# Feed-forward norm of a six-layer stack: by products across partitions, or token-major by transposes and statistics instructions in twelve slots

## The chip, the cores and the metric

The kernel runs on one core of a Trainium2 chip. The metric is the device time of one execution in microseconds (us). Three runs of the kernel before took 2170.97, 2175.17 and 2180.14 us, median 2175.17.

## What is computed

Four blocks follow each other on four batch elements of 512 tokens with 128 features: a linear attention, a stack of six layers, an attention with position slopes, and a gated network. The change lies in the second block. Its core in the reference:

```python
for i in range(DEPTH):            # 6
    x = attn_layer(shift_tokens(x), Wqkv[i], q_scale[i], k_scale[i], Wo[i]) + x
    x = ffn_layer(shift_tokens(x), ln_g[i], ln_b[i], W1[i], b1[i], W2[i], b2[i]) + x

def ffn_layer(x, g, bln, W1, b1, W2, b2):
    mu = x.mean(-1, keepdims=True)
    var = ((x - mu) ** 2).mean(-1, keepdims=True)
    xn = (x - mu) / jnp.sqrt(var + 1e-05) * g + bln
    a, gate = jnp.split(xn @ W1 + b1, 2, -1)
    return a * jax.nn.gelu(gate, approximate=False) @ W2 + b2
```

The attention layer has 16 heads of 64 features and windows of 32 tokens, of which each sees itself and the one before. The inner width of the feed-forward network is 341, taken as chunks of 128, 128 and 85 rows.

## The kernel before, in words

The stack keeps each batch element feature-major in a tile `z[b]`: 128 features on the partitions, the 512 tokens behind each other, the lower and the upper half of the features shifted against each other by one token (`halves`, L125).

The order of the stack is written out by hand (L643 to L705), as one loop over slots `s`; each engine runs its instructions in the order in which they are recorded. A step `k` is one half (8 heads) of one batch element in one layer, and takes four slots, one for each pair of heads. So a layer of four batch elements has 32 slots, and a group, one batch element's attention and feed-forward, has 8. In a slot the loop records, for the step that is `here`: the scores of a pair (`score`, L420: eight mask products of L429, then 32 small products of L439), the row maximum (`top`, L446, L448) on VectorE, eight exponentials with sums on ScalarE (L71 by way of L455), and at the slot's end the reciprocal (L463, VectorE) and the normalising product (L464, GpSimd). One slot later VectorE transposes the weights (L480) and SP issues eight DMAs that place them as `pT` (L490); two slots later TensorE forms the weighted values (L500), ScalarE copies them out (`attn`, L687), and in the slot after that they go through the output product (L508), which sums the eight pairs of a group in the PSUM tile `py` (L665, one buffer). Beside this, each slot does two projections of later steps (L323), whose results VectorE multiplies with the rotary table (L334) and ScalarE squares (L342); VectorE sums the squares (L354); GpSimd adds the rotated halves (L350); TensorE turns two earlier tiles (L395) and ScalarE copies the turns (L397); one value product (L405) is copied by ScalarE (`vn`, L409), and once in four slots SP moves the values (`ve`, L415 to L417). At the start of each fourth slot L363 clamps the sums and ScalarE takes a logarithm and an exponential.

PSUM: the score tile `sc` has a single buffer of two banks (L424). The products of projection, turn, value and feed-forward share four banks, tag `mm` (L287), which are given out in turn; a product waits until all readers of the tile that had its bank before are done.

The feed-forward of group g (`ff_part`, L513) is recorded at the end of the slots that follow its last output product, one part in each of seven slots. Recorded at the end of a slot, its instructions stand on each engine behind that slot's and ahead of the next slot's.

```python
done, part = divmod(s - 1, 8)
if 1 <= part and 1 <= done <= DEPTH * NB:
    ff_part(*divmod(done - 1, NB), part)
```

Part 1 (s mod 8 = 2): VectorE adds the output product to `z` (L517). Part 2 (3): TensorE multiplies by the centring matrix `cent` (L522), ScalarE takes the square (L524) and a copy with the scale g (L526). Part 3 (4): four one-column products with `mean_c` give the variance by token (L530), VectorE adds epsilon (L535), GpSimd raises to the power -0.5 (L536). Part 4 (5): four products spread it over the partitions (L540), VectorE multiplies (L545). Part 5 (6): three gate products (L550), and three gelus with a table load before and after. Part 6 (7): two up-products (L561), VectorE adds the bias and multiplies by the gelu (L565). Part 7 (0): the third one, the down-product (L571), and VectorE adds the result to `z` in two halves (L576). The next layer's projections of the same batch element begin at g*8 + 16.

The norm's own bias has no step of its own: `bias_late` (L291) multiplies it once for each layer by W1, twelve one-column products (L297), and three sums on VectorE (L304) make the six bias columns that parts 5 to 7 use. It stands in the layer's thirteenth slot (L622). `weights` (L615) records the loads of the next layer on SP; `par`, `w1` and `w2` have one buffer (L150, L617 to L621) and are loaded in the layer's tenth and eleventh slot.

In the last layer `residual` (L585) takes each batch element to the next block, in four parts after its feed-forward: GpSimd copies (L592), a centring product with square and copy (L595 to L597), the variance product with logarithm and exponential (L600 to L602), product and sum (L604, L605).

Of the kernel before, what the change touches and what calls it, by code (L numbers as in the profile page):

```python
# [32 lines left out]
def sandwich(ctx: ExitStack, tc: tile.TileContext, a: dict, out: bass.AP):  # L33
# [97 lines left out]
    with tc.tile_pool(name="a0w", bufs=1) as awp, tc.tile_pool(name="a0", bufs=4) as work, \  # L131
# [17 lines left out]
        for n in ("par", "w1", "w2"):  # L149
            loaded(0, n, a[f"f0_{n}"][0], bufs=1)  # L150
# [135 lines left out]
    with tc.tile_pool(name="f0", bufs=2) as work, \  # L286
# [4 lines left out]
        def bias_late(i):  # L291

            w = ws[i]
            pb = mm.tile([P, S], F32, tag="mm", name="pb")
            for k in range(6):
                h0, m = HCH[k % 3]
                nc.tensor.matmul(  # L297
                    pb[:m, k : k + 1],
                    lhsT=w["w1"][:, (k // 3) * DIN + h0 : (k // 3) * DIN + h0 + m],
                    rhs=w["par"][:, 5:6], start=True, stop=True,  # L300
                )
            w["bias"] = bias = wp.tile([P, 6], F32, tag="bias", bufs=1, name=f"bias_{i}")
            for c, m in ((0, P), (1, P), (2, HCH[2][1])):
                nc.vector.tensor_tensor(  # L304
                    bias[:m, c::3], pb[:m, c:6:3], w["par"][:m, 7 + c : 13 : 3], ALU.add
                )

# [91 lines left out]
        def value(k, t):  # L399
# [9 lines left out]
            nc.scalar.copy(o["vn"][:, t, :], pv)  # L409
# [100 lines left out]

        ff = {}

        def ff_part(i, b, part):  # L513
# [6 lines left out]
            elif part == 2:  # L520
                pc = mm.tile([P, S], F32, tag="mm", name="pc")
                nc.tensor.matmul(pc, lhsT=cent, rhs=zb[:, cur], start=True, stop=True)  # L522
                ff["sq"] = work.tile([P, S], F32, tag="ffsq", bufs=1, name="ffsq")
                nc.scalar.activation(ff["sq"], pc, AF.Square)  # L524
                ff["xg"] = work.tile([P, S], F32, tag="xg", bufs=1, name="xg")
                nc.scalar.activation(ff["xg"], pc, AF.Copy, scale=w["par"][:, 4:5])  # L526
            elif part == 3:
                pv = mm.tile([P, S], F32, tag="mm", name="pvar")
                for t in range(4):
                    nc.tensor.matmul(  # L530
                        pv[:, t : t + 1], lhsT=ff["sq"][:, t * P : (t + 1) * P], rhs=mean_c,
                        start=True, stop=True,
                    )
                rs = ff["rs"] = work.tile([P, 4], F32, name="rs")
                nc.vector.tensor_scalar_add(rs, pv[:, 0:4], 1e-5)  # L535
                nc.gpsimd.tensor_tensor(rs, rs, mhalf, ALU.pow)  # L536
            elif part == 4:
                pr = mm.tile([P, S], F32, tag="mm", name="prs")
                for t in range(4):
                    nc.tensor.matmul(  # L540
                        pr[:, t * P : (t + 1) * P],
                        lhsT=ff["rs"][:, t : t + 1].to_broadcast([P, P]),
                        rhs=ident, start=True, stop=True,
                    )
                nc.vector.tensor_tensor(ff["xg"], ff["xg"], pr, ALU.mult)  # L545
            elif part == 5:
                ff["gl"] = []
                for c, (h0, m) in enumerate(HCH):
# [6 lines left out]
                    table_act(gl[:m], pg[:m], AF.Gelu, bias=w["bias"][:m, 3 + c : 4 + c])  # L555
                    ff["gl"].append(gl)
            else:
                for c in ((0, 1), (2,))[part - 6]:
# [7 lines left out]
                        gl[:m], pa[:m], w["bias"][:m, c : c + 1], gl[:m], ALU.add, ALU.mult  # L566
                    )
                if part == 7:
                    py = mm.tile([P, S], F32, tag="mm", name="py")
                    for c, (_, m) in enumerate(HCH):  # L570
                        nc.tensor.matmul(  # L571
                            py, lhsT=w["w2"][:m, c, :], rhs=ff["gl"][c][:m, :],
                            start=(c == 0), stop=(c == 2),
                        )
# [576 lines left out]
```

## Time and profile before

| what | us |
|---|---|
| median of three runs | 2175.17 |
| the profiled execution | 2175.81 |
| its span, first to last instruction | 2174.1 |
| first slot's and last slot's scores begin | 127.3 and 1743.4 |
| TensorE busy | 1965.5 |
| ScalarE busy | 1671.6 |
| VectorE busy | 1574.3 |
| GpSimd busy | 1192.0 |

The profile is of one execution. PE is TensorE's products, PEld its weight loads, DVE VectorE, ACT ScalarE, POOL GpSimd, SPq the queue of SP. A line such as L446 is that of the kernel. In a row of the order in time, the first number is the start in us from the span's start, the second the duration, then engine, line, operation, output<-input, shapes, and in brackets the idle time of the engine just ahead and what ended it. A row of a stretch has the busy time of each engine and the number of its instructions, the granted TensorE clock (1.00 is full), the DMA share and GB/s. The chain is the work that ended last, followed backwards; its shares say which engine carried it.

### The profile page before, as it was taken

Reading aid. Unit: us, or ns where it says so; the run is one execution under the profiler, and the core shown is the slowest. Engines: PE = TensorE matmul, PEld = TensorE weight load, DVE = VectorE, ACT = ScalarE, POOL = GpSimd, SP = SyncE. Lnnn points to the kernel's source line nnn. Section 1 sums busy time; section 2 is a strip of 40 time slices with the busy share of each in tenths; the row PEclk is TensorE's granted clock in tenths of the full one; section 3 lists DMA queues with packets and bytes.
Section 4 is the critical chain, followed back from the end, with each engine's and each line's share of the span. In section 5 each row is a group of like instructions: output and inputs, shape, how many; then the busy total and the mean of one; then the engine's idle time right before and its main releaser. Section 6 shows DMA issues by size and latency. Waiting matters only on the chain.

```text
span 2174.1 us, 64681 instructions
## 1 busy us (share of the span) xinstructions
PE 1965.5 (90%) x25584; PEld 1098.2 (51%) x25584; DVE 1574.3 (72%) x2320; ACT 1671.6 (77%) x4786; POOL 1192.0 (55%) x1017
## 2 busy tenths in 40 slices
PE   6789999999999999999999999999999877788877
PEld 3245555555555565555555555555555533333323
DVE  3677777777777777877777777787777328888843
ACT  4477887887878788888888878888878636988973
POOL 1266566555664556645566555664555316888860
PEclk9799999999999999999999999999999987898898
DMA  2013322233221332213322133222221210000000
GB/s 91 0 36 89 96 64 74 56 91 94 65 72 52 93 96 67 72 53 95 95 65 73 52 94 95 66 72 53 80 70 53 74 36 20 1 1 1 1 0 20
DMA packets 98844, 129.40 MB, mean 60 GB/s; under 512 B 29552, under 2 KB 81520, under 8 KB 93936
## 3 DMA queue, kind: packets, MB, share of 16 engines
q1 hardware_dynamic: 98544, 125.27, 20.7%
q8 instruction: 204, 3.34, 0.7%
q14 instruction: 96, 0.79, 0.1%
HBM read 23.44 MB, written 1.05 MB: 11 GB/s over the span
## 4 chain that ended last, share of the span: by engine, by line
PE 48%; ACT 25%; DVE 16%; issue 4%; DMA 3%; SPq 3%; POOL 2%; ACTq 0%; POOLq 0%; DVEq 0%
ACT pr L71 11%; PE pp L323 8%; PE av L500 5%; PE pv L405 5%; PE py L508 4%; ACT sq L342 4%; PE tp L395 4%; PE sc L439 3%; PE py L571 3%; DMA pT<-blocks 3%; SPq L490 3%; PE pa L561 3%; ACT lb L71 2%; PE pg L550 2%; DVE la L850 2%
## 5 line engine op out<-in xcount | busy, mean ns | idle before, releaser
L350 POOL TENSOR_TENSOR r<-t 128x512 f32<-128x512 f32 x384 | 490.2, 1278 | 714.2 <-DVE t L334 601.9
L71 ACT ACTIVATE pr<-sc,top,rn 128x64 f32<-128x64 f32 x1536 | 607.9, 420 | 255.6 <-DVE top L448 233.6
L334 DVE TENSOR_TENSOR t<-pp,tab 128x1024 f32<-128x1024 f32 x384 | 466.8, 1215 | 11.1 <-PE pp L323 8.7
L354 DVE TENSOR_REDUCE ss<-sq 128x8 f32<-128x512 f32 x384 | 263.0, 685 | 227.5 <-ACT sq L342 227.3
L323 PE MATMUL pp<-wqkv,z 128*128 128x512 f32 x768 | 420.3, 631 | 6.6 <-ACT sq L342 6.3
L71 ACT ACTIVATION_READ_ACCUMULATOR pr<-sc,top,rn 128x1 f32 x1536 | 335.0, 218 | 0.0
L395 PEld LDWEIGHTS tp<-ident,r 128*128 128x128 f32 x1536 | 193.6, 142 | 206.5 <-issue 173.0
L342 ACT ACTIVATE sq<-pp 128x512 f32<-128x512 f32 x384 | 239.1, 623 | 34.6 <-DVE t L334 32.5
L395 PE MATMUL tp<-ident,r 128*128 128x128 f32 x1536 | 233.6, 275 | 0.9 <-ACT sq L342 0.9
L500 PE MATMUL av<-pT,vn 128*64 128x64 f32 x3072 | 194.0, 225 | 36.9 <-DMA pT<-blocks 36.6
L464 POOL TENSOR_TENSOR pr<-pr,den 128x512 f32<-128x512 f32 x192 | 200.7, 1045 | 45.5 <-DVE den L463 38.7
L405 PE MATMUL pv<-wqkv,z 128*128 128x512 f32 x384 | 219.4, 654 | 6.4 <-ACT sq L342 6.2
L508 PE MATMUL py<-attn,wo 128*128 128x512 f32 x384 | 200.6, 604 | 14.2 <-DVE z L517 12.5
L858 POOL TENSOR_TENSOR lb<-lb,la 128x2048 f32<-128x2048 f32 x40 | 182.2, 4556 | 53.0 <-issue 38.8
L500 PE MATMUL av<-pT,ve 128*64 128x64 f32 x3072 | 204.0, 229 | 2.7 <-DMA pT<-blocks 2.7
L380 POOL TENSOR_TENSOR r<-r,rn 128x512 f32<-128x512 f32 x192 | 197.0, 1049 | 0.0
L446 DVE TENSOR_REDUCE top<-sc 128x8 f32<-128x512 f32 x192 | 131.7, 686 | 87.2 <-PE sc L439 84.9
L323 PEld LDWEIGHTS pp<-wqkv,z 128*128 128x128 f32 x768 | 132.1, 192 | 120.2 <-issue 81.2
L500 PEld LDWEIGHTS av<-pT,vn 128*64 128x64 f32 x3072 | 161.7, 139 | 41.0 <-issue 30.9
L500 PEld LDWEIGHTS av<-pT,ve 128*64 128x64 f32 x3072 | 159.5, 138 | 38.8 <-issue 34.5
L439 PE MATMUL sc<-kT,qT 64*32 64x64 f32 x12288 | 166.3, 224 | 0.0
L439 PEld LDWEIGHTS sc<-kT,qT 64*32 64x32 f32 x12288 | 152.6, 106 | 0.0
(191 smaller groups left out, 3129.1 us busy)
## 6 DMA issues: line engine op xcount, KB each, us to landing
pT<-blocks SPq DMA_DIRECT2D x1536, 32.0 KB, 1.8
ve<-vn SPq DMA_DIRECT2D x48, 768.0 KB, 5.8
wqkv<-in_f_wqkv SPq DMA_DIRECT2D x36, 256.0 KB, 3.0
ve<-vn SPq DMA_DIRECT2D x48, 192.0 KB, 5.6
tab<-in_rot SPq DMA_DIRECT2D x12, 256.0 KB, 3.1
wo<-in_f_wo SPq DMA_DIRECT2D x6, 512.0 KB
ve<-vn SPq DMA_DIRECT2D x48, 64.0 KB, 5.2
w<-in_f_w SPq DMA_DIRECT2D x6, 341.0 KB
```

Source lines behind the costliest of these rows:

```text
L71: done = nc.scalar.activation(out, in_, func, **kw)
L323: nc.tensor.matmul(pp, lhsT=z[b][:, WIN + t * P : WIN + (t + 1) * P], rhs=ws[i]["qkv", hf][:, n * S : (n + 1) * S], start=True, stop=True,)
L334: nc.vector.tensor_tensor(t12, o["pp"].rearrange("p (h d) -> p h d", d=DH0).unsqueeze(1) .to_broadcast([P, 2, 8, DH0]), ws[i][f"tab{n}"][: ...
L342: nc.scalar.activation(sq, o["pp"], AF.Square)
L350: nc.gpsimd.tensor_tensor(r, t1, t2[:, :, ::-1, :], ALU.add)
L354: nc.vector.tensor_reduce(o["ss"][:, n, t, :], o["sq"].pop(j).rearrange("p (h d) -> p h d", d=DH0), AX.X, ALU.add,)
L395: nc.tensor.transpose(tp[:, p, :], flat[:, p * P : (p + 1) * P], ident)
L405: nc.tensor.matmul(pv, lhsT=z[b][:, WIN + t * P : WIN + (t + 1) * P], rhs=ws[i]["qkv", hf][:, 2 * S :], start=True, stop=True,)
L439: nc.tensor.matmul(scores[32 * w : 32 * w + 32, e, j, :], lhsT=o["qT"][rows, p, q0 : q0 + WIN], rhs=o["kT"][rows, p, q0 : q0 + KW], start= ...
L464: nc.gpsimd.tensor_tensor(o["pr"], o["pr"], o["den"].unsqueeze(3).to_broadcast([P, 2, 4, KW]), ALU.mult)
L500: nc.tensor.matmul(av[64 * e : 64 * e + 64, q0 : q0 + 64], lhsT=vs[c][:, j, (2 * p + e) * DH0 : (2 * p + e + 1) * DH0], rhs=pT[:, c, :, 4 ...
L508: nc.tensor.matmul(py, lhsT=ws[i]["wo"][:, c, :], rhs=t, start=(c == 0), stop=(c == 7))
```

## The change

The norm becomes token-major. Part 2 turns the four token blocks of `z` by four transposes on TensorE, and ScalarE copies them to a tile `xt` (tokens on the partitions). Part 3 takes mean and variance by four bn_stats and four bn_aggr instructions on VectorE; epsilon and power stay. The new part 4 subtracts the mean and multiplies by the norm, four instructions on VectorE. The new part 5 turns back, four transposes, and ScalarE copies out with g as scale and the norm's bias as bias. Gates, up-products and down-product follow as parts 6 to 9; the first is as before but for its bias, which comes straight from `par`. `bias_late` is gone.

Parts and the four parts of the residual have a list of their slots, counted from 8*g: 2, 3, 5, 7, 8, 9, 11, 13, 14, and 15 to 18. So two groups overlap, and by s mod 8 the parts stand at 2 (part 1), 3 (part 2 and, of the group before, part 7), 5 (3 and 8), 6 (9), 7 (4), 0 (5) and 1 (6). The loop runs five slots longer. In the slot of the gates (s mod 8 = 1) the copies `attn` and `vn` are on VectorE in place of ScalarE. `par`, `w1` and `w2` have two buffers.

```diff
-            loaded(0, n, a[f"f0_{n}"][0], bufs=1)
+            loaded(0, n, a[f"f0_{n}"][0])
...
-        def bias_late(i):
...
-            nc.scalar.copy(o["vn"][:, t, :], pv)
+            copy(o["vn"][:, t, :], pv)
...
+        LATE = (2, 3, 5, 7, 8, 9, 11, 13, 14, 15, 16, 17, 18)
...
             elif part == 2:
-                pc = mm.tile([P, S], F32, tag="mm", name="pc")
-                nc.tensor.matmul(pc, lhsT=cent, rhs=zb[:, cur], start=True, stop=True)
-                ff["sq"] = work.tile([P, S], F32, tag="ffsq", bufs=1, name="ffsq")
-                nc.scalar.activation(ff["sq"], pc, AF.Square)
-                ff["xg"] = work.tile([P, S], F32, tag="xg", bufs=1, name="xg")
-                nc.scalar.activation(ff["xg"], pc, AF.Copy, scale=w["par"][:, 4:5])
+                pt = mm.tile([P, 4, P], F32, tag="mm", name="pt")
+                for t in range(4):
+                    nc.tensor.transpose(
+                        pt[:, t, :], zb[:, WIN + t * P : WIN + (t + 1) * P], ident
+                    )
+                ff["xt"] = work.tile([P, 4, P], F32, tag="xt", bufs=1, name="xt")
+                nc.scalar.copy(ff["xt"], pt)
             elif part == 3:
-                pv = mm.tile([P, S], F32, tag="mm", name="pvar")
+                st = work.tile([P, 4, 6], F32, tag="st", bufs=1, name="st")
+                ff["mv"] = mv = work.tile([P, 4, 2], F32, tag="mv", bufs=1, name="mv")
                 for t in range(4):
-                    nc.tensor.matmul(
-                        pv[:, t : t + 1], lhsT=ff["sq"][:, t * P : (t + 1) * P], rhs=mean_c,
-                        start=True, stop=True,
-                    )
+                    nc.vector.bn_stats(out=st[:, t, :], in_=ff["xt"][:, t, :])
+                for t in range(4):
+                    nc.vector.bn_aggr(out=mv[:, t, :], in_=st[:, t, :])
                 rs = ff["rs"] = work.tile([P, 4], F32, name="rs")
-                nc.vector.tensor_scalar_add(rs, pv[:, 0:4], 1e-5)
+                nc.vector.tensor_scalar_add(rs, mv[:, :, 1], 1e-5)
                 nc.gpsimd.tensor_tensor(rs, rs, mhalf, ALU.pow)
             elif part == 4:
-                pr = mm.tile([P, S], F32, tag="mm", name="prs")
                 for t in range(4):
-                    nc.tensor.matmul(
-                        pr[:, t * P : (t + 1) * P],
-                        lhsT=ff["rs"][:, t : t + 1].to_broadcast([P, P]),
-                        rhs=ident, start=True, stop=True,
-                    )
-                nc.vector.tensor_tensor(ff["xg"], ff["xg"], pr, ALU.mult)
+                    nc.vector.tensor_scalar(
+                        ff["xt"][:, t, :], ff["xt"][:, t, :], ff["mv"][:, t, 0:1],
+                        ff["rs"][:, t : t + 1], ALU.subtract, ALU.mult,
+                    )
             elif part == 5:
+                px = mm.tile([P, 4, P], F32, tag="mm", name="px")
+                for t in range(4):
+                    nc.tensor.transpose(px[:, t, :], ff["xt"][:, t, :], ident)
+                ff["xg"] = work.tile([P, S], F32, tag="xg", bufs=1, name="xg")
+                nc.scalar.activation(
+                    ff["xg"], px.rearrange("p t c -> p (t c)"), AF.Identity,
+                    bias=w["par"][:, 5:6], scale=w["par"][:, 4:5],
+                )
+            elif part == 6:
...
-            for s in range(-8, LAST + 14):
+            for s in range(-8, LAST + LATE[-1] + 1):
...
+                copy = nc.scalar.copy
+                if s % 8 == LATE[5] % 8 and LATE[5] < s:
+                    copy = nc.vector.tensor_copy
...
-                    nc.scalar.copy(attn, av)
+                    copy(attn, av)
...
+                for part, late in enumerate(LATE, 1):
+                    g, left = divmod(s - late, 8)
+                    if left or not 1 <= g <= DEPTH * NB:
+                        continue
+                    if part < 10:
+                        ff_part(*divmod(g - 1, NB), part)
+                    elif g > NB * (DEPTH - 1):
+                        residual((g - 1) % NB, part - 9)
```

## The prediction

> **What bounds the kernel now.** I read four views in this order: busy times and chain on the page, busy time by stretch over one cycle of eight slots, the order of VectorE, ScalarE and TensorE instructions inside that cycle, and the waits. Only the stack (127 to 1743 us of the span) is touched, and the passage to the next layer behind it.
>
> ```profile
> PE 1965.5 (90%) x25584; PEld 1098.2 (51%) x25584; DVE 1574.3 (72%) x2320; ACT 1671.6 (77%) x4786; POOL 1192.0 (55%) x1017
> PE 48%; ACT 25%; DVE 16%; issue 4%; DMA 3%; SPq 3%; POOL 2%; ACTq 0%; POOLq 0%; DVEq 0%
> ```
>
> TensorE looks like the bound, but only half of the chain is its own. The second view shows why: one cycle, a row for each slot from its first mask product, here s mod 8 = 4, 5, 6, 7, 0, 1, 2, 3.
>
> ```profile
> core 0: us, PE busy (x) PEld busy (x) DVE busy (x) ACT busy (x) POOL busy (x), PEclk, DMA share, GB/s
> 900.40:907.94 7.54, 7.54 (x129) 5.18 (x129) 6.63 (x12) 7.51 (x27) 3.29 (x3) 1.00 0.14 37
> 907.94:915.50 7.56, 7.56 (x129) 5.11 (x128) 5.78 (x11) 6.59 (x24) 7.27 (x7) 1.00 0.56 156
> 915.50:926.10 10.60, 9.44 (x127) 5.24 (x126) 6.62 (x10) 9.19 (x27) 7.21 (x8) 1.00 0.22 56
> 926.10:934.50 8.40, 8.40 (x125) 4.77 (x124) 5.30 (x8) 8.37 (x26) 2.90 (x3) 1.00 0.08 22
> 934.50:944.80 10.30, 10.30 (x137) 5.46 (x138) 8.50 (x16) 7.09 (x25) 4.93 (x5) 1.00 0.14 38
> 944.80:951.70 6.90, 6.75 (x129) 4.14 (x129) 5.98 (x9) 4.26 (x19) 2.74 (x4) 1.00 0.63 164
> 951.70:959.20 7.50, 6.83 (x128) 4.22 (x128) 5.93 (x9) 6.13 (x23) 5.71 (x7) 1.00 0.15 40
> 959.20:967.60 8.40, 7.77 (x130) 4.46 (x131) 6.75 (x11) 6.31 (x23) 3.69 (x4) 1.00 0.13 34
> sum 67.20, PE 64.58 PEld 38.58 DVE 51.50 ACT 55.44 POOL 37.73; mean PE 8.07 PEld 4.82 DVE 6.44 ACT 6.93 POOL 4.72
> ```
>
> A slot without feed-forward work takes 6.68 us of TensorE by the chain's pieces (mask and scores 0.89, projections 1.06 and 0.86, two turns of 0.44, output 0.86, weighted values 1.08, value 1.05). Slots 7, 0, 4 and 5 are that plus their own products. Slots 1, 2, 3 and 6 hold 2.6 us in which TensorE waits. The third view shows what it waits for in slots 1 to 3; the lines are of VectorE, ScalarE, TensorE.
>
> ```profile
> 946.42 0.69 DVE L446 TENSOR_REDUCE top<-sc 128x8 f32<-128x512 f32 x1
> 952.62 0.69 DVE L354 TENSOR_REDUCE ss<-sq 128x8 f32<-128x512 f32 x1 [0.77 <-ACT sq L342]
> 953.23 0.68 DVE L446 TENSOR_REDUCE top<-sc 128x8 f32<-128x512 f32 x1
> 953.94 0.87 DVE L448 TENSOR_TENSOR top<-top,rn 128x8 f32<-128x8 f32 x1
> 960.72 1.37 DVE L517 TENSOR_TENSOR z<-z,py 64x512 f32<-64x512 f32 x2
> 962.13 0.69 DVE L446 TENSOR_REDUCE top<-sc 128x8 f32<-128x512 f32 x1
> ```
>
> ```profile
> 947.44 0.40 ACT L71 ACTIVATE pr<-sc,top,rn 128x64 f32<-128x64 f32 x1 [4.19 <-DVE top L448]
> 951.93 0.66 ACT L342 ACTIVATE sq<-pp 128x512 f32<-128x512 f32 x1
> ```
>
> ```profile
> 951.67 0.30 PE L429 MATMUL sc<-mask,identb 64*32 64x256 bf16 x8 [0.15 <-ACT pr L71]
> 959.16 0.30 PE L429 MATMUL sc<-mask,identb 64*32 64x256 bf16 x8 [0.67 <-ACT pr L71]
> 962.25 1.10 PE L508 MATMUL py<-attn,wo 128*128 128x512 f32 x2 [0.63 <-DVE z L517]
> ```
>
> There is a second clock, a ring of VectorE and ScalarE. The row maximum (top, at T) releases the first exponential (A = T + 1.02). ScalarE needs 5.15 from there to the end of the second square, VectorE's sum of it is behind that, and the next maximum is behind the sum: 5.79 after A, so 6.81 from top to top (946.42 to 953.23). What VectorE does at a slot's end is added: 1.4 for z at 960.72. And as the score tile is single, the next scores start 4.23 after A (951.67, 959.16). So a slot lasts the longer of TensorE's work and lag + 4.23. All my sums use these two clocks.
>
> **The change, part by part.** *TensorE products.* Taken out per group: centring 0.86, variance 0.79, spreading 0.89 (chain pieces), 2.54. Added: eight transposes. The row is the turn (L395), four of the same form in 0.44 on the chain, so 0.88; saved 1.66. The Trainium skill speaks against that (TensorE: Matmul & The Clock Gate, Part 4: PE-mode transpose): a transpose costs about 275 ns in a kernel and transposes may not hold the clock up. By it eight cost 2.2 and 0.34 is saved. The record of one turn here is 275 ns too, but four end in 0.44 and the clock column beside them reads 1.00; I take 0.88.
>
> *ScalarE and GpSimd.* Square 0.69 and scaled copy 0.78 go, a copy of 0.6 and a scaling of 0.66 come; GpSimd's power (1.03) moves from slot 4 to slot 5 and is needed two slots later: nothing, under waits of 1.3 and more in each of these slots.
>
> *Layer bias.* bias_late goes: twelve one-column products and three sums a layer. The cycles that hold it take 70.1, 68.2, 68.1, 68.0 and 70.1 us (stretches between first mask products) where plain ones take 67.15: together 9 us. The table's second buffer costs nothing: the same DMAs leave SP at the same slots, and without it their loads would wait for the later readers.
>
> *Spreading.* By slot mod 8 the feed-forward work becomes 0: back-transpose and scaling; 1: gates; 2: first sum into z; 3: transpose and two up-products; 5: statistics and third up-product; 6: down-product and z; 7: scaling by the norm. I go round once, from slot 7 (lag = T from the slot's start).
> - 7: z is written after the down-product as in slot 1 now, so lag 1.65, A 2.67, length 2.67 + 4.23 = **6.9** (TensorE 6.68 waits).
> - 0: the ring brings 8.46, then four scalings and the clamp L363 (0.37 mean). One 128-wide VectorE step: 512 wide takes 0.61 start to start (952.62 to 953.23), 0.53 of it elements, so 0.13 + 0.08 = 0.21 for 128; the scaling (SBUF only) at the rate of L765's 481 ns for 512 about 0.14. That makes 0.55. It must also pass GpSimd: L448 took 0.87 instead of 0.17 when GpSimd was busy. The Trainium skill (SBUF — State Buffer, Who interferes with whom) agrees, and says that a tensor_scalar in a two-port form is held up in the same way, for a whole GpSimd instruction. By L448's mean (0.32) one such wait is 0.15, by the rule up to 1.28 (L350); I take 0.4. T = 8.46 + 1.3 - 6.9 = 2.9, A 3.9, length **8.1** (TensorE 7.12).
> - 1: T 1.5, A 2.6 to 2.7. The second gate product takes the bank of the second projection, free after the square (A + 5.15 = 7.8; four banks in turn), restarts at 0.24 more (1.10 against 0.86 at L508): 7.85 + 0.24 + 1.72 = **9.8**. ScalarE's copies of attn and value (1.0) go to VectorE, 2 x 0.62; reciprocal and second sum queue behind them, and behind these GpSimd's normalising; all are needed only in slot 2, over 1 us later. So hidden; without that cover 1.2.
> - 2: the last gelu follows the last gate product by 0.7, then the table load 1.28: A 2.1, TensorE bound, **6.75**.
> - 3: z adds 1.4: T 2.55, A 3.6. L508 waits 0.3 with its restart. The first up-product is now third behind pv and needs the second projection's bank: 3.6 + 5.15 = 8.75, + 0.24 + 1.72 = **10.7**. TensorE's own work is 8.84: here 1.9 is lost.
> - 4: T 1.1, **6.7**. 5: T 1.3, A 2.4, **7.55**.
> - 6: statistics. The trace has no such instruction. Lower bound for one: 0.21 (128 elements), aggregate 0.09 (L535, 128x4, is 0.15 as a record). Upper: 0.5 and 0.3, two passes. I take the lower, nearest to the reduction's row: 0.84 + 0.36 + 0.1, + gl 0.67, + 0.2 port: 2.2. T = 2.4 + 5.79 + 2.2 - 7.55 = 2.85. The length stays today's: the down-product equals the gates, and the DMA wait stays (the third ve transfer holds SP's queue from 911.86 to 914.16, the pT transfers issue only from 914.27, and av waits 1.4 for them): **10.6**.
>
> Sum 67.1 against 67.2. So the 1.66 saved on TensorE, and the calmer slots 0 and 7, are spent in slots 1 and 3, where products come to banks that the ring frees late. 23 cycles x -0.1 = -2.
>
> *Passage behind the stack.* The last groups are five slots longer. Now 44.8 us pass from the last scores (1743.5) to x (1788.2). Before the last output come the third group's gates and residual product, 2.58 + 0.86 = +3.4; what they replace (pa, py at 1754 to 1759) lay under the wait for pT. From z (1764.0) to the gates (1770.8) it takes 6.8 now; then transposes 0.65, three up-products of the other group 2.6, gl 0.7, statistics 1.4, gl 0.7, down-product 1.1, z 1.5, scaling 0.8, transposes and copy 1.3: 10.8, a little of it overlapping: +3.3. The other residual's logarithm and table load come between: +2. Together +8 (bounds 3 and 11).
>
> Sum: 2175.8 - 2 - 9 + 8 = 2172.8, against the profiled execution's 2175.81 (span 2174.1, 1.7 around it); the median is 0.6 lower. So **2172**.
>
> **Rivals.** *TensorE is the bound after all*: ring and banks do not bite in 0, 1 and 3. These slots shrink to 7.3, 9.3 and 9.3, cycle 64.7, -2.5 x 23 = -57, with -1: 2117. For it: 90% busy; against: the waits of slots 1 to 3. Half of it (one of the bank waits missing) gives about 2148. *Slower: the statistics delay the maximum of slot 6.* At the upper costs slot 6 gets 2.0 + 1.2 + 0.1 + 0.67 + 0.4 = 4.4 in place of 2.2, so T 5.0, A 6.1; the value product needs the bank that the first square frees (A + 2.1 = 8.2) before 1.05 + 2.58: 11.9, +1.3 x 23 = +30: 2202. It decides from about 2.8 at the end of slot 5 on, when A + 2.1 passes 7.1, the end of today's DMA wait. *The two copies do nothing*: then slot 2 starts its exponentials 1.0 later, slot 3 too: +20, 2192.
>
> **Numbers.** Main case, within 0.5% (about what a measurement of this kernel can tell from no change, 11 us): 0.46. First rival 0.08 in full and 0.17 by half: faster 0.25. Slower by statistics 0.21, by copies 0.08: slower 0.29. The range leaves out the full first rival and little above the slow one: 2142 to 2204.
>
> **What would show it.** Slots 0 to 7 near 8.1, 9.8, 6.75, 10.7, 6.7, 7.55, 10.6, 6.9. The first up-product waits for ScalarE's square or copy, scores wait for pr in slots 7 and 0; statistics about 0.3 as records; TensorE busy some 45 us less; about 53 us from the last scores to x. I am wrong if up-products in slot 3 do not wait, if slot 6 passes 11 us, or if records of the scalings are mostly above 0.5.

## The result, and the profile after the change

The changed kernel takes 2179.8 us (median of 20 runs, 2170.3 to 2192.0), the kernel before 2175.4 (20 runs beside them): a ratio of 1.0019, 95% interval 1.0003 to 1.0034. The forecast of 2172 had the size of the change about right, next to nothing, and its sign wrong: by the interval the change costs 1 to 7 us, where 3 were to be saved. The profiled execution has a span of 2179.3 us, 5.3 more than before.

The page of the changed kernel, its busy times and the chain by engine:

```profile
PE 1924.5 (88%) x25272; PEld 1055.7 (48%) x25272; DVE 1634.9 (75%) x2611; ACT 1655.7 (76%) x4741; POOL 1191.6 (55%) x1017
PE 37%; ACT 26%; DVE 21%; SPq 5%; issue 5%; DMA 5%; POOL 1%; ACTq 0%; DVEq 0%; POOLq 0%
```

TensorE has 41 us less to do, close to the forecast (45), and its share of the chain falls from 48% to 37%. The shares that grew are those of VectorE (16% to 21%), of SP's queue (3% to 5%) and of DMA (3% to 5%). In the mean of the 23 cycles TensorE has 1.8 us less work in each, and is idle for 1.7 us more (4.6 in place of 2.9). One cycle by stretch, rows for s mod 8 = 4, 5, 6, 7, 0, 1, 2, 3, as in the forecast's table:

```profile
core 0: us, PE busy (x) PEld busy (x) DVE busy (x) ACT busy (x) POOL busy (x), PEclk, DMA share, GB/s
897.17:903.85 6.68, 6.68 (x123) 4.06 (x122) 6.20 (x11) 5.17 (x21) 1.28 (x1) 1.00 0.12 27
903.85:911.51 7.66, 7.66 (x124) 4.47 (x123) 5.98 (x10) 6.32 (x23) 6.19 (x6) 1.00 0.56 153
911.51:922.61 11.10, 9.47 (x127) 5.30 (x126) 8.03 (x19) 7.49 (x25) 8.27 (x9) 1.00 0.22 51
922.61:929.52 6.91, 6.75 (x121) 4.15 (x121) 5.95 (x9) 4.24 (x19) 1.37 (x2) 1.00 0.08 19
929.52:937.82 8.30, 7.47 (x126) 4.75 (x125) 7.42 (x16) 6.64 (x25) 3.46 (x3) 1.00 0.15 37
937.82:947.48 9.66, 9.51 (x127) 5.03 (x126) 7.78 (x13) 9.26 (x27) 7.98 (x8) 1.00 0.52 139
947.48:954.70 7.22, 6.75 (x121) 4.14 (x121) 4.54 (x7) 7.19 (x23) 3.43 (x5) 1.00 0.18 41
954.70:965.31 10.61, 9.33 (x128) 5.25 (x127) 8.22 (x13) 8.50 (x27) 5.68 (x5) 1.00 0.14 34
sum 68.14, PE 63.62 PEld 37.17 DVE 54.13 ACT 54.80 POOL 37.67; mean PE 7.95 PEld 4.65 DVE 6.77 ACT 6.85 POOL 4.71
```

TensorE is idle for 4.5 us of this cycle, most of it in slots 6, 3 and 0. Outside the first two cycles and the last, seven slots have the same length in almost every cycle (slots 4, 5, 7, 0, 1, 2, 3: 6.68, 7.6, 6.90, 8.30, 9.65, 7.22, 10.60); slot 6 alone varies, mostly from 10.1 to 11.9 (13.7 once, where the granted clock is at half for 3.4 us), with a mean of 10.9.

Where the 5.3 us come from, by the stretches between first mask products (forecast beside it). The last mask product is that of the last slot; the passage is taken to the end of the copy L590 (L597 before) of the last batch element:

| stretch | forecast | measured |
|---|---|---|
| ahead of the first slot (127.3 to 124.9) | 0 | -2.3 |
| 23 cycles (67.81 to 67.73 in the mean) | -2 and -9 | -2.0 |
| the slots ahead of and behind them | 0 | -1.2 |
| passage: last mask product to that copy (40.2 to 49.3) | +8 | +9.1 |
| the rest of the kernel | 0 | +1.7 |
| sum | -3 | +5.3 |

The 23 cycles hold the miss. Part of the comparison is the clock's: from the second cycle to the 22nd, the profile of before has four stretches of 3.4 us in which the granted clock is at half, that of the changed kernel one. Slot 5 of the kernel before, in two cycles that both hold the layer bias, without and with such a stretch:

```profile
773.51:781.08 7.57, 7.57 (x130) 5.11 (x128) 5.31 (x12) 5.61 (x22) 6.59 (x8) 1.00 0.60 163
498.79:508.04 9.25, 9.25 (x130) 5.91 (x129) 5.83 (x11) 6.50 (x23) 7.30 (x7) 0.82 0.51 139
```

A cycle with one is 2 to 3 us longer than its like, so without them the 23 cycles would be some 4 us longer after the change, not 2 shorter (an estimate from these two profiles).

Three readings of the trace point at where the time is lost. The first is ScalarE from the end of slot 1 into slot 2 (start, duration, engine, line, operation):

```profile
945.35 0.67 ACT L325 ACTIVATE sq<-pp 128x512 f32<-128x512 f32 x1
946.03 1.28 ACT L67 ACT_TABLE_LOAD   x1
947.32 1.83 ACT L71 ACTIVATE gl<-pg,par 128x512 f32<-128x512 f32 x3
949.17 1.28 ACT L67 ACT_TABLE_LOAD   x1
950.47 0.41 ACT L71 ACTIVATE pr<-sc,top,rn 128x64 f32<-128x64 f32 x1
```

The table load stands behind the second square, three gelus behind it, the second load behind them: 4.44 us in one line, and the first exponential of slot 2 comes 2.99 after the slot's start (947.48), not 2.1. With 4.23 more the slot is 7.22.

The second is SP's queue in slots 4 to 6, first in the changed kernel, then in the kernel before (slot 4 starts at 897.17 and at 900.41):

```profile
901.20 4.94 SPq L473 DMA_DIRECT2D pT<-blocks  x8
906.24 0.96 SPq L398 DMA_DIRECT2D ve<-vn  x1
...
907.89 2.23 SPq L400 DMA_DIRECT2D ve<-vn  x1
910.23 5.23 SPq L473 DMA_DIRECT2D pT<-blocks  x8
```
```profile
905.08 5.46 SPq L490 DMA_DIRECT2D pT<-blocks  x8
...
911.86 2.30 SPq L417 DMA_DIRECT2D ve<-vn  x1
914.27 10.92 SPq L490 DMA_DIRECT2D pT<-blocks  x16
```

In both, the queue is busy with hardly a gap from slot 4's transfers of pT through the three ve to slot 5's pT, which slot 6 needs. The third is TensorE, where that pT is waited for in slot 6, and where the first up-product of slot 3 waits for ScalarE:

```profile
918.02 0.34 PE L483 MATMUL av<-pT,vn 128*64 128x64 f32 x4 [1.63 <-DMA pT<-blocks]
...
963.40 1.98 PE L554 MATMUL pa<-xg,w 128*128 128x512 f32 x4 [0.64 <-ACT kT L380]
```

### The profile page after: what moved, and what is told of

Same layout as the page of the kernel before. It is cut to its first block, busy times and chain, and to the rows that moved or that the text cites. A ratio compares the mean times of both kernels' runs of the same rounds, so it can differ in the third digit from the quotient of the medians.

```text
span 2179.3 us, 64331 instructions
## 1 busy us (share of the span) xinstructions
PE 1924.5 (88%) x25272; PEld 1055.7 (48%) x25272; DVE 1634.9 (75%) x2611; ACT 1655.7 (76%) x4741; POOL 1191.6 (55%) x1017
## 3 DMA queue, kind: packets, MB, share of 16 engines
HBM read 23.44 MB, written 1.05 MB: 11 GB/s over the span
## 4 chain that ended last, share of the span: by engine, by line
PE 37%; ACT 26%; DVE 21%; SPq 5%; issue 5%; DMA 5%; POOL 1%; ACTq 0%; DVEq 0%; POOLq 0%
ACT pr L71 12%; PE pp L306 6%; SPq L473 5%; ACT sq L325 4%; DMA pT<-blocks 4%; PE av L483 4%; PE pv L388 4%; PE py L564 3%; PE pa L554 3%; PE sc L422 3%; PE tp L378 3%; PE py L491 3%; DVE ss L337 2%; DVE top L429 2%; DVE la L847 2%
## 5 line engine op out<-in xcount | busy, mean ns | idle before, releaser
L317 DVE TENSOR_TENSOR t<-pp,tab 128x1024 f32<-128x1024 f32 x384 | 466.9, 1216 | 10.8 <-PE pp L306 7.7
L447 POOL TENSOR_TENSOR pr<-pr,den 128x512 f32<-128x512 f32 x192 | 200.6, 1045 | 51.4 <-DVE den L446 49.5
```

What stands on the lines that cost most here:

```text
L317: nc.vector.tensor_tensor(t12, o["pp"].rearrange("p (h d) -> p h d", d=DH0).unsqueeze(1) .to_broadcast([P, 2, 8, DH0]), ws[i][f"tab{n}"][: ...
L447: nc.gpsimd.tensor_tensor(o["pr"], o["pr"], o["den"].unsqueeze(3).to_broadcast([P, 2, 4, KW]), ALU.mult)
```

## The experiments

Ratios are to runs of the kernel before on the same chip, in brackets their 95% interval; times are medians. Slot lengths are medians of 23 cycles of the profiled execution.

**The queue as the clock of slots 4 to 6.** The values are copied in two portions:

```diff
-if t == 3:
-    nc.sync.dma_start(out=ve[0:96], in_=vn[0:96])
+if t == 2:
+    nc.sync.dma_start(out=ve[0:96, 0:3], in_=vn[0:96, 0:3])
     nc.sync.dma_start(out=ve[96:P, 1:4], in_=vn[96:P, 0:3])
+if t == 3:
+    nc.sync.dma_start(out=ve[0:96, 3], in_=vn[0:96, 3])
     nc.sync.dma_start(out=ve[96:P, 0], in_=vn[96:P, 3])
```

> The changed kernel, but the copy of the values (ve) is sent in two portions: three quarters of it one slot earlier (in slots 0 and 4), only the last quarter after the last value product. Theory (SP's queue is the clock of slots 4 to 6): from slot 4's start the queue sends pT (5 us), ve (3.9), pT (5), so slots 4, 5 and 6 together last about 25.2 us whatever TensorE does; with ve's rest at about 1.3 us slot 6 falls from 10.9 to TensorE's 9.3 to 9.6, 23 x -1.4 = -32 us: about 2147. Rival (VectorE's statistics set slot 6, as the slower rival of the prediction has it): slot 6 stays at 10.5 or more, 2175 to 2182.

Measured: 2152.1 us, 0.9902 (0.9887 to 0.9918). Slot 6 falls from 10.8 to 10.1, its mean from 10.9 to 9.95, and stops varying upward. The queue was the clock of slot 6, worth some 1 us a cycle. (The first slot starts 3 us earlier in this profile too; but in three of the runs below with the same edit it starts at 124.3 to 124.8, as without it, so that part is not put down to the edit.) But TensorE's 9.3 was not reached: in slot 6 there is no wait for pT any more, and in its place

```profile
902.03 1.13 PE L388 MATMUL pv<-wqkv,z 128*128 128x512 f32 x2 [0.81 <-ACT sq L325]
```

the value product waits for the bank that ScalarE's first square frees, which is late because the maximum is late: the mechanism of the forecast's slower rival, hidden until now behind the queue.

**The same edit in the kernel before.**

> The kernel before with the values sent in two portions, as in the experiment on the changed kernel. Theory (SP's queue is the clock of slots 4 to 6 in both kernels, and no statistics stand in the way in this one): slot 6 goes from 10.6 to TensorE's 9.5, 23 x -1.1 = -25 us: 2149, about where the changed kernel with the same edit is (2152); the change is then neutral with and without the queue. Rival (the queue binds only in the changed kernel): 2172 to 2178.

Measured: 2168.9 us, 0.9970 (0.9955 to 0.9984): close to the rival, and the theory fell in its size. Slot 6 went from 10.5 to 9.3 as it had, but slot 7 from 8.6 to 9.4. There the gates stand in slot 6, and ScalarE's line of table load, gelus, table load runs into slot 7. To test this, gelu and table loads were left out beside the edit:

> The kernel before with the values sent in two portions and Identity in the place of the gelu (no table loads, a linear gate). With the split alone slot 6 fell by 1.2 us and slot 7 rose by 0.8. Theory (in that kernel ScalarE's line of square, table load, gelus, table load is the next clock behind the queue: an earlier slot 6 only makes slot 7 wait for it): slot 7 goes back to 8.4 or less with slot 6 at 9.3, 23 x -1.0 = -23 us on the split alone: 2146. Rival (slot 7 is held by something else): 2164 to 2172.

Measured: 2142.0 us, 0.9835 (0.9816 to 0.9855); slots 6 and 7 at 9.3 and 8.4. So in the kernel before, queue and gelus lay beside each other, and a shorter queue alone had little to give; the change moved the gates away from there. The gelu left out alone, with the queue as it was, was not run.

**ScalarE's line in slot 2.** Gelu without its table loads, and the two copies of slot 1 back on ScalarE:

```diff
-table_act(gl[:m], pg[:m], AF.Gelu, bias=w["par"][:m, 10 + c : 11 + c])
+nc.scalar.activation(gl[:m], pg[:m], AF.Identity, bias=w["par"][:m, 10 + c : 11 + c])
```
```diff
-copy = nc.vector.tensor_copy
+copy = nc.scalar.copy
```

> The changed kernel with Identity in the place of the gelu, so that the two table loads of a group (1.28 us each) are left out; the gate is then linear. Theory (in slot 2 the exponentials wait for table load, three gelus and table load one after another, A = 2.99 where the prediction had 2.1): slot 2 goes from 7.22 to 6.75, and slot 3 starts its exponentials 0.4 earlier and goes from 10.6 to 10.2; together -0.9 x 23 = -20 us: 2160. Rival (slot 2 is held by something else than the gelus, such as the two copies on VectorE): both slots stay, 2177 to 2182.

> The changed kernel with the two copies of slot 1 (attn and vn) on ScalarE, as in all other slots. Theory (ScalarE's line of square, table load, gelus, table load holds slot 2; the copies stand ahead of the table load): exponentials of slot 2 start 1.0 later, A = 4.0, slot 2 goes from 7.22 to 8.2, slot 3 keeps its length; 23 x 1.0 = +23 us: 2203. Rival (the copies cost VectorE as much as they save ScalarE): 2176 to 2184.

Measured: 2159.7 us, 0.9940 (0.9917 to 0.9963), slot 2 at 6.68 and slot 3 at 10.18; and 2199.9 us, 1.0105 (1.0081 to 1.0129), slot 2 at 8.17. Both ends of the theory are met to a few us. Moving the copies to VectorE is worth 20 us, the size of the forecast's third rival; slot 2 alone pays it, slot 3 keeps its length (10.59).

**The layer bias**, `bias_late` and its calls taken out of the kernel before:

```diff
-bias_late(0)
-elif i > 0 and at == 12:
-    bias_late(i)
```

> The kernel before without the layer bias: bias_late is left out, the gates take the bias column of the parameters as it is, so the part of it that comes from the norm's shift is missing. Theory (the bias is worth what the cycles with it are longer): five cycles 69.2 against 67.4 without it, 9, and 2 ahead of the first slot: about -10 us, 2165. Rival (those cycles are long by the weight loads that fall into them): at most -3 us, 2172.

Measured: 2163.6 us, 0.9957 (0.9940 to 0.9974), 9.4 us. Its five cycles fall from 69.2 to 67.9 in the mean, and the first slot starts 2.3 us earlier. The changed kernel keeps both gains (67.8 in the same places, first slot at 124.9). But two of the five cycles of before hold a stretch at half clock, some 2 us each: the profile shows 3 us for the bias in these cycles and 2.3 ahead of them. Where the rest of the 9.4 lies (6 to 13 by the interval) is open.

**The statistics.** First twice as many, then one quarter of them with the queue out of the way:

```diff
-for t in range(4):
+for t in (0, 1, 2, 3, 0, 1, 2, 3):
     nc.vector.bn_stats(out=st[:, t, :], in_=ff["xt"][:, t, :])
```
```diff
-for t in range(4):
-    nc.vector.bn_stats(out=st[:, t, :], in_=ff["xt"][:, t, :])
+nc.vector.bn_stats(out=st[:, 0, :], in_=ff["xt"][:, 0, :])
...
```

> The changed kernel with each of the four statistics instructions issued twice (the second writes the same values), +0.85 us on VectorE at the end of slot 5. Theory (SP's queue is the clock of slot 6): T of slot 6 goes from 3.2 to 4.05 and A to 5.1, the value product's bank is free at 7.2 against 7.5 for the end of the weighted values: 0 to +4 us, 2180 to 2184. Rival (the statistics set slot 6): +0.85 x 23 = +20 us: 2200.

> The changed kernel with the values sent in two portions, and the statistics of the first quarter of the tokens alone, used for all four (three statistics and three aggregates left out, about 1 us of VectorE at the end of slot 5). Theory (with the queue out of the way the statistics hold slot 6 at 10.1): slot 6 falls to TensorE's 9.3 to 9.4, 23 x -0.75 = -17 us on the split alone: 2135. Rival (something else holds 10.1): 2150 to 2154.

Measured: 2186.0 us, 1.0054 (1.0040 to 1.0068), slot 6 now at 11.08 (10.95 to 11.35 in 21 of 23 cycles); and 2152.2 us, 0.9886 (0.9870 to 0.9902), no gain on the split alone. Twice the statistics add 6 to 8 us, a little over the theory's 0 to 4 and not 20: as long as the queue is later they are hidden, and only what passes it counts. But with the queue out of the way slots 5 and 6 together last 17.7 with four statistics and with one. My theory of the second run fell. VectorE and, last, GpSimd in that run show why:

```profile
897.33 0.28 DVE L518 BATCH_NORM_STATS2 st<-xt 128x6 f32<-128x128 f32 x1
897.87 1.05 DVE L521 TENSOR_SCALAR rs<-mv 128x4 f32<-128x4 f32 x1
```
```profile
897.84 2.05 POOL L363 TENSOR_TENSOR r<-r,rn 128x512 f32<-128x512 f32 x2
```

The add of 1e-5 to four numbers takes 1.05 us and ends at 898.92, just as the first of GpSimd's two instructions (1.04 each, from 897.84) ends. In 23 of 24 groups it ends 0.02 to 0.03 us after a GpSimd instruction; so it does in the changed kernel, where it is 0.44 long in the mean. The time that three statistics took is now spent waiting. The test is to take the GpSimd instruction away, beside the split and the single statistic:

```diff
-normed(scale[0], 2 * scale[1])
-normed(scale[0], 2 * scale[1] + 1)
```

> The changed kernel with values in two portions and one statistic, and without GpSimd's scaling of the turned keys by their norm (two instructions of 1.04 us in slots 0, 1, 4 and 5 left out, so the keys are not normalised). Theory (VectorE's add of 1e-5, and its product of the maxima, wait at the port for the end of a GpSimd instruction, mostly this one; the statistics' time was only covered by it): slots 5 and 6 together go from 17.7 to TensorE's 16.9 to 17.0; slot 0, whose four scalings take 1.48 us where about 0.6 would do, from 8.3 to 7.4 to 7.6; 23 x -1.6 = -37 us on the split alone: 2115. Rival (the port is not it; ScalarE or TensorE hold slots 5 and 6): these two stay at 17.7, time 2140 or more.

Measured: 2133.7 us, 0.9807 (0.9791 to 0.9823). The groups of instructions, with the key scaling and without (total busy, mean ns of one):

```profile
L521 DVE TENSOR_SCALAR rs<-mv 128x4 f32<-128x4 f32 x24 | 20.1, 838 | 0.8
```
```profile
L521 DVE TENSOR_SCALAR rs<-mv 128x4 f32<-128x4 f32 x24 | 4.7, 197 | 0.8
```

Slots 5 and 6 fall to 17.0, within 0.3 of TensorE's own time, and the value product's wait in slot 6 is gone. That half of the theory holds, shown with one statistic: the GpSimd instruction, the theory's port, was what stood behind the queue. The other half does not: slot 0 stays at 8.2, its four scalings at 434 ns in the mean. Here and in the changed kernel, only the first of four meets a GpSimd instruction, and that is the normalising (L448; L447 in the changed kernel), which the edit leaves in. In the changed kernel the first and the third of four, and what stands beside the first:

```profile
931.08 0.71 DVE L526 TENSOR_SCALAR xt<-xt,mv,rs 128x128 f32<-128x128 f32 x1
931.97 0.34 DVE L526 TENSOR_SCALAR xt<-xt,mv,rs 128x128 f32<-128x128 f32 x1
930.66 1.04 POOL L447 TENSOR_TENSOR pr<-pr,den 128x512 f32<-128x512 f32 x1
```

So of the 1.49 us that four take, some 0.38 are waiting; the rest is their own time.

**Place against port.** Statistics and scalings ahead of the second sum of squares, beside the values in two portions, with nothing left out:

```diff
+for part in (3, 4):
+    g, left = divmod(s - LATE[part - 1], 8)
+    if not left and 1 <= g <= DEPTH * NB:
+        ff_part(*divmod(g - 1, NB), part)
 if rot:
     squared(rot[0], 2 * rot[1] + 1)
```

> The changed kernel with values in two portions, and VectorE's statistics (slot 5) and scalings (slot 7) issued ahead of the slot's second sum of squares, where VectorE waits 0.8 us for ScalarE's square, not behind it. Nothing is left out. Theory (what VectorE does behind that sum delays the next maximum, what it does ahead of it uses the wait): slot 6 falls from 10.1 to 9.4, slot 0 from 8.3 to 7.7; 23 x -1.3 = -30 us on the split alone: 2122. Rival (the port holds these instructions wherever they stand, and now the sum behind them too): 2145 to 2155.

Measured: 2155.6 us, 0.9909 (0.9895 to 0.9924): the rival. Slot 6 gained 0.3, slot 0 lost 0.5: the four scalings took 0.73 us in the mean in place of 0.45, because two of them meet a GpSimd instruction there (1.17 and 1.08 us; the other two 0.33, as before). With the scalings on ScalarE, in the changed kernel, the products for the bias on GpSimd:

```diff
-nc.vector.tensor_scalar(
-    ff["xt"][:, t, :], ff["xt"][:, t, :], ff["mv"][:, t, 0:1],
-    ff["rs"][:, t : t + 1], ALU.subtract, ALU.mult,
+nc.scalar.activation(
+    ff["xt"][:, t, :], ff["xt"][:, t, :], AF.Identity,
+    bias=ff["nm"][:, t : t + 1], scale=ff["rs"][:, t : t + 1],
 )
```

> The changed kernel with the four scalings by the norm on ScalarE (scale and bias by token, in slot 0's first wait of ScalarE) in place of VectorE; minus the mean times the norm is worked out on GpSimd by two small products at the end of slot 6. Nothing is left out. Theory (slot 0 is long because the scalings take 1.5 us of VectorE, two thirds of it waiting at the port, ahead of its maximum; ScalarE waits 1.3 us there and has no such port): slot 0 falls from 8.3 to TensorE's 7.15, -1.15 x 23 = -26 us on 2180: 2154. Rival (ScalarE's scalings stand ahead of its exponentials and put them off as much): slot 0 at 8.0 or more, 2173 or more.

Measured: 2172.6 us, 0.9978 (0.9962 to 0.9995), slot 0 at 7.97: mostly the rival. The maximum came 1.0 earlier, but ScalarE needs 1.7 us for the four and the exponentials start only 0.3 earlier. Slot 0 falls by as much, and slot 1 grows by 0.3. That two thirds of the scalings' time was waiting, as expected here, was wrong: it was a quarter (0.38 of 1.49).

**Other places for the products.** One slot earlier for all from the up-products on:

```diff
-LATE = (2, 3, 5, 7, 8, 9, 11, 13, 14, 15, 16, 17, 18)
+LATE = (2, 3, 5, 7, 8, 9, 10, 12, 13, 14, 15, 16, 17)
```

> The changed kernel with the up-products and all that follows one slot earlier (two up-products in slot 2 in place of 3, the third in slot 4 in place of 5, down-product in slot 5 in place of 6). Theory (the products of slot 3 come to a bank that the ring frees late, and slots 4 to 6 have one queue clock of 22.3 us without the down-product in slot 6): slots 0 to 7 near 8.3, 9.65, 9.2 (second up-product waits for the second square), 8.1, 7.55, 9.3, 6.9, 6.7, sum 65.7 against 67.7: -2.0 x 23 = -46 us: 2134. Rival (TensorE's products cost the same wherever they stand, what is gained in 3 and 6 is lost in 2 and 5): 2172 to 2184.

Measured: 2145.9 us, 0.9857 (0.9838 to 0.9876), 1.6% under the changed kernel. Slots 0 to 7: 8.29, 9.66, 8.75, 7.99, 7.53, 9.72, 8.23, 6.79. Slots 2 to 4 as foretold or better; slot 5 0.4 over its 9.3, and slot 6 1.3 over its 6.9, because the statistics, their add (0.4 us beside GpSimd) and z now stand in a row ahead of its maximum. 12 us of the theory's 46 are missing. Four variants of it add nothing:

> Both edits: parts one slot earlier and values in two portions. Theory: once the down-product has left slot 6 the queue (22.3 us for slots 4 to 6) is under the other clocks (23.7), so the split adds little: 0 to -6 us on the kernel with the moved parts, 2128 to 2134. Rival (the queue still binds): a further -20 us.

> The kernel with the moved parts (up-products in slots 2 and 4, down-product in 5), and the statistics at the end of slot 4 in place of 5. In that kernel slot 6 takes 8.2 us because the statistics and z stand one behind the other on VectorE ahead of its maximum. Theory (VectorE's work at a slot's end delays the next maximum, and what the next slot has of TensorE work hides it): slot 6 falls to 6.9, slot 5 grows from 9.6 to at most 10.2, because its value product waits for the bank of the first square; -0.8 x 23 = -18 us on 2146: 2128. Rival (the wait only moves, slot 5 grows by what slot 6 loses): 2142 to 2150.

> The kernel with the moved parts (up-products in slots 2 and 4, down-product in 5), with statistics and scalings ahead of the second sum of squares. Nothing is left out. Theory: slot 6 falls from 8.2 to 7.5, slot 0 from 8.3 to 7.7; 23 x -1.3 = -30 us on 2146: 2116. Rival (the port holds them wherever they stand): 2140 to 2150.

> The kernel with the moved parts (up-products in slots 2 and 4, down-product in 5) and the scalings on ScalarE. Nothing is left out. Theory: the two gains lie in different slots and add: slot 0 falls from 8.3 to 7.15, -26 us on 2146: 2120. Rival: what slot 0 gains slot 1 gives back, because its second gate product waits for the bank of the second square: 2140 or more.

Measured: 2147.5 us, 0.9868 (0.9848 to 0.9888), so the queue no longer binds; 2152.3, 0.9878 (0.9859 to 0.9896), slot 6 at 6.9 as foretold but slot 5 at 11.2, where the value product waits 1.3 for the first square; 2151.2, 0.9897 (0.9881 to 0.9912); and 2145.6, 0.9862 (0.9837 to 0.9888), slot 0 at 7.96 and slot 1 at 9.95. The rivals were right in the last three of the four, to some 2 us.

**The passage behind the stack.** The norm of the last group by the old chain (centring, square, variance, power, spreading):

```diff
+old = i == DEPTH - 1 and b == NB - 1
+if old and part == 2:
+    pc = mm.tile([P, S], F32, tag="mm", name="pc")
+    nc.tensor.matmul(pc, lhsT=cent, rhs=zb[:, cur], start=True, stop=True)
...
```

> The changed kernel with the norm of the very last group (of 24) done as in the kernel before: centring product, square, variance products, power, spreading product, and the shift added on ScalarE. Theory (of the 9 us that the passage behind the stack grew, 3.9 is the longer chain from z to the gates: statistics, scalings and two sets of transposes where nothing hides them): 10.7 from z to the gates goes back to about 7.5, passage 49.3 to 46, time -3: 2177. Rival (the passage is longer by the later slots of the parts alone, not by the norm): passage within 1 us of 49.3.

Measured: 2184.0 us, 1.0039 (1.0028 to 1.0050); passage 51.0. As built, the up-products of the group ahead read, and wait 1.3 us for, the last group's input; without this wait the passage would be 49.7, no shorter than with the new norm: the rival. What lies between z and the gates is seen on TensorE in the changed kernel:

```profile
1760.53 0.63 PE L509 MATMUL pt<-ident,z 128*128 128x128 f32 x4 [1.57 <-DVE z L502]
1761.00 2.74 PE L554 MATMUL pa<-xg,w 128*128 128x512 f32 x6
...
1769.22 1.09 PE L533 MATMUL px<-ident,xt 128*128 128x128 f32 x4 [2.46 <-DVE xt L526]
...
1771.18 2.84 PE L543 MATMUL pg<-xg,w 128*128 128x512 f32 x6
```

10.7 us from the transposes to the gates (6.8 before), and 5.6 of them are the other group's up- and down-products, which the later slots put there. They count although TensorE waits behind them, because VectorE works in order: its scalings (1768.37) stand behind the other group's z, which waits for the down-product:

```profile
1766.80 1.53 DVE L569 SCALAR_TENSOR_TENSOR z<-py,par,z 64x512 f32<-64x512 f32 x2 [1.22 <-PE py L564]
1768.37 1.55 DVE L526 TENSOR_SCALAR xt<-xt,mv,rs 128x128 f32<-128x128 f32 x4
```

With the up-products and all that follows one slot earlier the passage is 44.7, so the order of the products explains about half of what it grew.

## Why the forecast was wrong

Step by step, in its own order; slot lengths as means of 23 cycles.

- *TensorE products.* Right. 41 us less busy (45); the product behind four transposes starts 0.44 to 0.47 us after the first of them where it does not wait, at a clock of 1.00, so 0.88 and not 2.2 was the sum to make.
- *Layer bias.* 9.4 us (9), right in size and partly by luck. The 9 were read from cycles alone, and in two of the five cycles, those of 70.1, it was a stretch at half clock that made them 2 us longer than the other three; without them the reading would have been 5. The 2.3 that the bias costs ahead of the first slot were left out.
- *Slots 7, 0, 4, 5.* 6.9, 8.2, 6.7, 7.6 against 6.9, 8.1, 6.7, 7.55. Right, in slot 0 by other terms: the wait for GpSimd is the 0.4 of the forecast (0.38), but a scaling starts 0.26 us after the one before, not 0.14, so four took 1.49 as against 0.55 + 0.4; the clamp took less (0.22 for 0.37).
- *Slots 1 and 3.* 9.57 and 10.37 (typically 9.65 and 10.60, less in the first and last cycles) against 9.8 and 10.7: nearly right, by two errors that cancel. Exponentials start 0.4 later than forecast in each (A 3.0 and 4.0), but the bank that the product needs is the second turn's, freed by ScalarE's copy (A + 4.65), not the second projection's (A + 5.15). The waits are there, which excludes the first rival. In the mean the two slots give 13 us in 23 cycles, which hides as much of what slots 2 and 6 lost.
- *Slot 2: "The last gelu follows the last gate product by 0.7, then the table load 1.28: A 2.1".* This step failed. The gates' products are not what the gelus wait for: ScalarE must first finish the square of slot 1 (A + 5.15), then load, three gelus, load. A is 2.99, the slot 7.22 in place of 6.75. The run without gelu and that with the copies on ScalarE showed it from both sides. The row was in the trace of before, at the start of its slot 7, where TensorE's work hid it; from table load to exponential are the same 4.45 us:

```profile
923.67 0.60 ACT L409 COPY vn<-pv 128x512 f32<-128x512 f32 x1
924.29 1.28 ACT L67 ACT_TABLE_LOAD   x1
925.59 1.83 ACT L71 ACTIVATE gl<-pg,bias 128x512 f32<-128x512 f32 x3
927.44 1.28 ACT L67 ACT_TABLE_LOAD   x1
928.74 0.41 ACT L71 ACTIVATE pr<-sc,top,rn 128x64 f32<-128x64 f32 x1
```

  In the mean the slot was 0.66 over, 15 us in 23 cycles; 0.48 in the median, the rest being the first cycle.
- *Slot 6: "The length stays today's ... and the DMA wait stays".* This step failed too. The wait stays, but it was anchored to the wrong point: the queue runs from slot 4's transfers on, so it fixes the time from these to the end of slot 6, not the length of slot 6. Slot 4 became 0.92 us shorter (7.60 to 6.68, medians), its transfers start only 0.65 earlier in it (4.68 to 4.03 after its start), and the rest comes back in slot 6 as waiting: 10.77 in place of 10.47. In the mean it is 10.9 in place of the forecast's 10.6, 7 us in 23 cycles, of which 3 are the one cycle with a stretch at half clock. The split of the values showed that the queue holds the slot.
- *Statistics.* Instructions of the size forecast: 278 ns as records (about 0.3), four in 0.86, four aggregates in 0.36. The 0.2 for the port was about its mean in the changed kernel (0.44 for an add that takes 0.20 alone), but not its bound: the add waits for the end of a GpSimd instruction. The Trainium skill's rule (SBUF — State Buffer, Who interferes with whom), an exclusive lock of the shared port pair, that the forecast had weighed for the scalings and cut to a third, describes this add to 0.03 us, and puts its bound at GpSimd's 1.04, not at a mean wait. In the changed kernel it costs nothing as long as the queue is later (10.8 against 10.1).
- *Passage.* +9.1 against +8; the forecast's three terms, 3.4, 3.3 and 2, add up to 8.7, of which it took 8. The later slots were rightly seen; but the old norm's chain does not bring the time back, and the order of the two groups' products brings back half of it. By the forecast's own marks, from the last scores to x, it is 54.1 (53).
- *The sum.* The cycles came out at 67.73 for 67.1, 14 us too many; those of before are 67.81 where the forecast reckoned with 67.2 and 9 us of bias, 5 too few. Those 5 are about what the two other cycles with a stretch at half clock (69.65 and 69.42) are over their like. What is left of this, 9 us, less the 3.5 gained at both ends of the stack, plus 1 in the passage and 1.7 behind it, is the 8 us by which the forecast missed.

The forecast said it would be wrong "if slot 6 passes 11 us": it did so in 9 of 23 cycles. That 10.6 was a mark on the queue's clock and not on the slot's could be read in the trace of before: there, too, the queue was busy from slot 4's transfers on. The other two signs stayed out: up-products in slot 3 do wait, and 28 of 96 scalings took more than 0.5 us.

## What to carry to other kernels

A wait has an origin: write down where the chain that ends it begins, and when the slots between are shortened, move the wait with that beginning, or part of what is saved in one slot will be waited for two slots later (here 0.3 us of 0.92). Count an in-order engine's line from the last thing ahead of it, table loads included, not from the operand that one instruction needs. And behind each clock that is taken away stands the next: here the queue held slot 6 at 10.8 us, the add beside GpSimd at 10.1, TensorE at 9.3. Moving products to slots with room (2145.9 us, 0.9857) gave more than any other single edit that leaves nothing out. And before two profiles are compared by cycles, count the stretches at half clock in each.

## What the hardware showed

- A VectorE instruction over four numbers (128x4, f32) can take 1.05 us: in 23 of 24 cases its end follows GpSimd's by 0.02 to 0.03 us. Leaving work out ahead of it only lengthened it (0.44 to 0.84 in the mean); leaving out the GpSimd instruction shortened it to 0.20.
- A scaling of 128x128 on VectorE takes 0.34 us with GpSimd idle, and 0.71 when it starts beside a GpSimd instruction. Moved to a place where VectorE waited for ScalarE, two of four met GpSimd and took 1.17 and 1.08.
- What a transfer costs in SP's queue differs with what was sent ahead: the third ve transfer, 64 KB, holds the queue for 2.23 us behind 768 and 192 KB, and the last one of the same size for 0.59 when these went a slot earlier.
- A stretch of 3.4 us at half clock made a slot of the same TensorE products 9.25 us long in place of 7.57.
